# Layer 1 with one adapter per batch in four column slots, and eight value gathers moved behind the key gathers

## The chip, the core and the metric

The kernel runs on one core of one Trainium2 chip. The metric is the device time of one execution, in microseconds (us). All engines of the core work at the same time, each on its own list of instructions: TensorE (PE in the profile) for matmuls and transposes through an identity, VectorE (DVE), ScalarE (ACT), GpSimd (POOL), and SyncE (SP), which here only issues transfers. They wait for each other through semaphores.

## The reference, cut to what matters

The input x is 8 batches of 128 tokens with 512 features, in f32. Four layers follow each other, each as `x = x + ffn(cond(x))`. Layer 0 is a gated feed-forward with adapters, layer 2 an attention over a paged cache, layer 3 a routed mixture. The change lies in layer 1 and in the first steps of layer 2. Layer 1 is:

```python
B_sel = B[adapter_ids]                       # one adapter of 8 for each batch
A_sel = A[adapter_ids]
Bx  = einsum('bni,bri->bnr', x, B_sel)       # 512 features -> 16 ranks
y   = einsum('bnr,bor->bno', Bx, A_sel)      # 16 ranks -> 512, scaling 1
scores = 8 * softmax(y @ Wr.T + br)          # 8 experts, all used
low = einsum('bsd,hrd->bshr', y, A1)         # 8 experts x 16 ranks
x   = x + 2 * einsum('bshr,hor,bsh->bso', low, B1, scores)
```

In layer 2 each batch has 512 cached keys and values for each of 8 key heads, gathered row by row through a block table, and 32 query heads.

## The kernel before

The state is x, transposed: 128 partitions by 4 chunks of features by 1024 tokens. Tokens are worked on in two halves of 512 (`g` = 0, 1; `TG` = 2, and `HB` = 4 batches in each half).

**The gate stage (layer 0)** runs 11 blocks of feed-forward rows (`f` = 0 to 10, 13.4 us each). In each block, PE works through seven products for both halves, DVE and ACT evict them, POOL forms sums of the next weights (L484) after SP has loaded them (L98). Between the two parts of a block, a few prepared DVE operations are taken from generators (L615 to L617): `tables` (L200) makes index tables from the integer inputs in blocks 1 and 2, `turned_by_parts` (L360) turns weights 32 by 32 on DVE in blocks 3 to 6. What it turns is written out by SP to DRAM with the blocks exchanged and loaded back. Its scratch is rows of the big tile `h` that later blocks overwrite with their evictions. These instructions keep the order in which they are written (`kept`).

**Layer 1** does not form y. The two weights behind it that depend on no token are multiplied once into `w11` (L648): 128 rows, which are 8 adapters times 16 ranks, by 136 columns, which are 8 experts times 16 ranks and 8 router columns. Its parts, by half:

- `adapt(g)` (L771): all 8 adapters' ranks for all 512 tokens, four matmuls of 128x512 into one bank of PSUM; then DVE multiplies by `mask1` (L325, L327), which leaves for each batch the 16 rows of its own adapter and zeroes the other 112. The result is `t1`, called `l` in the profile as part of the tile `l1`.
- `mids1(g)` (L250): `t1` of each batch times `w11`, four matmuls of 128 tokens by 136 (`midp`), two in a bank, copied out by ACT (L259).
- `route1(g)`: softmax on DVE with one Exp on ACT, and the mixing weights applied (`mw`).
- `mix1(g)` (L306): four transposes on PE, copied out by ACT as `midT`.
- `outs1(g)`: four matmuls of 128x512 with `wB1` (`eo`), each added to x by DVE (L323).

Layer 0 ends with the same parts (`mix0`, `mids0`, `outs0`) and a base product, so that one of its four `eo` blocks for a half takes ten passes. The parts of both layers are interleaved by hand (L783 to L801) so that PE has work of one while DVE and ACT route the other. `small_bank` has two PSUM banks in turn and `large_bank` three.

**The attention (layer 2)** starts inside this. `att.begin` (L1365) loads weights and lets POOL gather the keys and values of step 0 (8 + 8 indirect gathers of 128 rows, L999). `att.begun` (L1372) turns those keys on DVE after the first `adapt`, and gathers the keys of step 1 into the same tiles. `att.first` (L1378) projects steps 0 and 1 with seven products each (`q_one`, `q_six`, `q_five`, L1056) and rotates the queries and keys on POOL (`vq`, `vk`, L1155) and DVE. `run` (L1408) goes over 32 steps of two batches and one key head: scores, Exp, sums, values (`av`), output product, and the projection two steps ahead. In its step 0, after the first half of the sums, it gathers the values of step 1 (L1473). POOL's instructions and those after the start of `first` keep their written order.

An f32 matmul appears in the profile as two passes.

Of the kernel before, what the change touches and what calls it, by code (L numbers as in the profile page):

```python
# [17 lines left out]
P = 128  # L18
NB = 8
# [28 lines left out]
def forward(ctx: ExitStack, tc: tile.TileContext, a: dict, out: bass.AP):  # L48
# [3 lines left out]
    def mm(o, lhsT, rhs, start, stop):  # L52
# [30 lines left out]
    down_turned, adapter_turned = (  # L83
        nc.dram_tensor(n, (rows_, P), F32, kind="Internal").ap() for n, rows_ in (("AdT", FF), ("wb1T", D))
# [109 lines left out]
    mask1 = const.tile([P, NB], F32, tag="mask1", name="mask1")  # L194
# [5 lines left out]
    def tables():  # L200
# [3 lines left out]
        yield dve.tensor_scalar(mask1, ids1, p_div16, None, ALU.is_equal)  # L204
# [34 lines left out]
    def experts(tag, wmr, topk, mult, bias, wB, base, yT, evac, mid_of=None, width=136):  # L239
# [5 lines left out]
        def operands(tok):  # L245
            if mid_of:
                return mid_of(tok)
            return [(yT[:, c, tok], wmr[:, c, :]) for c in range(DC)]

        def mids(g, bank):  # L250
            m = sm.tile([P, HB, width], F32, tag="mid", name=f"mid_{tag}_{g}")
            for j in range(HB // 2):
                ps = bank([P, 2, width], f"midp_{tag}_{g}_{j}")
                for i in range(2):
                    t0 = (g * HB + 2 * j + i) * P
                    ops = operands(slice(t0, t0 + P))
                    for k, (l, r) in enumerate(ops):
                        mm(ps[:, i, :], l, r, k == 0, k == len(ops) - 1)
                act.copy(m[:, 2 * j : 2 * j + 2, :], ps)  # L259
            M[g] = m  # L260
# [64 lines left out]
    def block_masked(dst, ps, mask, g):  # L325

        return dve.tensor_tensor(  # L327
            dst.rearrange("p (b t) -> p b t", t=P),
            ps.rearrange("p (b t) -> p b t", t=P),
            mask[:, 4 * g : 4 * g + 4].unsqueeze(2).to_broadcast([P, 4, P]),  # L330
            ALU.mult,
        )


# [6 lines left out]
    with c0:  # L341
# [18 lines left out]
        def turned_by_parts(h):  # L360

            spare = h[:, NF - 2 : NF, :].rearrange("p f t -> p (f t)")
            half = 672
# [7 lines left out]
            kept(sp.dma_start(h[:, NF - 3, 0:D], a["wb1"]))  # L371
            yield dve.transpose(h[:, NF - 3, D : 2 * D], h[:, NF - 3, 0:D])
            for q in range(4):
                kept(sp.dma_start(
                    adapter_turned.rearrange("(b i) (q j) -> q i b j", i=32, j=32)[q],
                    h[32 * q : 32 * q + 32, NF - 3, D : 2 * D].rearrange("i (b j) -> i b j", j=32),
                ))
# [235 lines left out]
        for f in range(1, NF):  # L613
            after = f + 1 < NF and weight_sums(f + 1, gate_weights(f + 1))
            gates_by_seven(f, A, itertools.chain(  # L615
                itertools.islice(tabled, 15) if f < 3 else itertools.islice(angles, 3),
                itertools.islice(turning, 3 <= f < 7),  # L617
# [134 lines left out]
    with psa:  # L752
# [13 lines left out]
        l1 = att.scratch([P, DC * P + NT], "l1")  # L766
        wa1 = l1[:, 0 : DC * P].rearrange("p (c r) -> p c r", c=DC)
        sp.dma_start(wa1, chunks(a["wa1"]))
        t1 = l1[:, DC * P : DC * P + NT]

        def adapt(g):  # L771
            tok = slice(g * 512, (g + 1) * 512)
            ps = small_bank([P, 512], f"t1_{g}")
            for c in range(DC):
                mm(ps, wa1[:, c, :], x[:, c, tok], c == 0, c == DC - 1)
            return block_masked(t1[:, tok], ps, mask1, g)
# [3 lines left out]
            mid_of=lambda tok: [(t1[:, tok], w11)],  # L780
# [8 lines left out]
        outs0(1, (0, 1), large_bank)  # L789
        adapted = adapt(0)  # L790
        outs0(1, (2, 3), large_bank)
        mids1(0, small_bank)
        route1(0)
        att.begin()
        att.begun(adapted)
        adapt(1)
        mix1(0, small_bank)
        outs1(0, range(DC), large_bank)
        mids1(1, small_bank)
# [78 lines left out]
def attention(tc, a, x, ident, lens, kvrow, part, ww, wop, ypool, sums, rot, eps, psa, c2, chunks, mm):  # L878
# [493 lines left out]
    def begun(behind):  # L1372
# [3 lines left out]
        gather(1, "k")  # L1376

# [30 lines left out]
    def run(pool_, end_of, bank, keep):  # L1408
# [20 lines left out]
        for n, (qd, p) in enumerate(steps):  # L1429
# [41 lines left out]
            if n == 0:  # L1471
# [984 lines left out]
```

## Time and profile before

| | us |
|---|---|
| median of 3 runs | 1470.01 |
| lowest, highest | 1468.61, 1470.76 |
| the profiled execution | 1471.33 |
| its span, first to last instruction | 1469.5 |
| PE busy in it | 1456.8 |
| DVE, POOL, ACT busy | 1066.5, 854.4, 557.5 |
| layer 1's first projections on PE (L53, `t`), 16 passes | 7.3 |
| its second steps (L53, `midp` from `w` and `l`), 16 passes | 2.4 |

The profile gives the start and length of each instruction, merged where equal ones follow each other ("x8"). Matmuls overlap: their mean length is longer than the distance between two starts, and what PE is held for is read from start to start. In brackets stands how long an engine stood idle before a group and what released it; "issue" means that the profile shows nothing that it waited for.

### The profile page before, as it was taken

The numbers are of one execution on the slowest core, as the hardware profiler recorded it, in microseconds if no ns is written. First come the engines' busy times: TensorE is split into PE (matmuls) and PEld (weight loads), VectorE is DVE, ScalarE is ACT, GpSimd is POOL, SyncE is SP. The second block draws the span as 40 slices with busy tenths as digits, with TensorE's granted clock in tenths as the row PEclk, the third lists the DMA queues.
The fourth block names the chain that finished last, engine by engine and source line by source line (L and its number), as shares of the span: only waits on it lengthen the run. The fifth ranks groups of instructions, "written<-read, shape, count | busy, mean of one in ns | idle before, by whom it ended". The sixth has DMA issues, their size and how long they took to land.

```text
span 1469.5 us, 17710 instructions
## 1 busy us (share of the span) xinstructions
PE 1456.8 (99%) x5313; PEld 919.3 (63%) x5313; DVE 1066.5 (73%) x2132; ACT 557.5 (38%) x1415; POOL 854.4 (58%) x877
## 2 busy tenths in 40 slices
PE   9999999999999999999999999999999999999997
PEld 7888786455555555555565555555555555557886
DVE  4675535488888887877778787777878888874575
ACT  1111101044545544454455444445544444532110
POOL 2241104477777777777677777767777776731310
PEclk9999999999999999999999999999999999999999
DMA  7430312214646544555444456445445644564001
GB/s 245 131 76 26 73 36 70 90 38 114 186 136 189 155 113 132 154 168 145 139 146 119 131 150 177 130 139 153 123 132 147 174 138 141 134 166 128 1 12 49
DMA packets 210600, 180.17 MB, mean 123 GB/s; under 512 B 85888, under 2 KB 180320, under 8 KB 210368
## 3 DMA queue, kind: packets, MB, share of 16 engines
q1 hardware_dynamic: 191888, 141.61, 34.9%
q0 software_dynamic: 17056, 36.49, 8.1%
q8 instruction: 45, 0.74, 0.2%
q10 hardware_dynamic: 1552, 0.85, 0.2%
q14 instruction: 59, 0.48, 0.1%
HBM read 133.94 MB, written 44.68 MB: 122 GB/s over the span
## 4 chain that ended last, share of the span: by engine, by line


## 5 line engine op out<-in xcount | busy, mean ns | idle before, releaser
L999 POOL DMA_INDIRECT kn<-in_k_cache,kvrow_k x256 | 271.0, 1059 | 77.5 <-issue 71.2
L999 POOL DMA_INDIRECT vals<-in_v_cache,kvrow_v x256 | 272.4, 1064 | 73.6 <-issue 60.7
L1307 PE MATMUL av<-pT,vals 128*128 128x512 f32 x640 | 290.6, 592 | 0.2 <-DVE oT L1317 0.2
L1259 ACT ACTIVATE pT<-st,hide 128x512 f32<-128x512 f32 x256 | 175.9, 687 | 190.2 <-PE st L1255 165.8
L1255 PE MATMUL st<-qT,kT 128*128 128x512 f32 x512 | 235.6, 592 | 0.0
L1307 PEld LDWEIGHTS av<-pT,vals 128*128 128x128 f32 x640 | 121.4, 190 | 153.1 <-issue 149.7
L1155 POOL TENSOR_TENSOR vq<-q,txq 128x256 f32<-128x256 f32 x128 | 121.1, 976 | 130.8 <-ACT sqq L1129 87.1
L1255 PEld LDWEIGHTS st<-qT,kT 128*128 128x128 f32 x512 | 97.1, 190 | 108.7 <-issue 105.6
L1275 DVE TENSOR_TENSOR part<-pT 128x512 f32<-128x512 f32 x128 | 88.2, 690 | 81.6 <-ACT pT L1259 70.9
L1056 PE MATMUL q_one<-q,x 128*128 128x384 f32 x256 | 93.0, 486 | 0.0
L1129 ACT ACTIVATE sqq<-q 128x128 f32<-128x128 f32 x252 | 78.3, 311 | 10.5 <-DVE q L1105 3.9
L1056 PEld LDWEIGHTS q_one<-q,x 128*128 128x128 f32 x256 | 48.5, 190 | 39.8 <-issue 14.1
L1056 PE MATMUL q_six<-q_s,xs_all 128*128 128x384 f32 x192 | 69.8, 486 | 0.0
L1110 ACT COPY q<-q_one 128x256 f32<-128x256 f32 x32 | 11.9, 372 | 151.8 <-PE q_one L1056 133.4
L1056 PE MATMUL wo_one<-o,oT 128*128 128x256 f32 x256 | 65.7, 379 | 0.0
L1255 PE MATMUL st<-qT,kTn 128*128 128x512 f32 x128 | 65.4, 592 | 0.0
L1056 PE MATMUL wo_two<-o_s,os 128*128 128x256 f32 x256 | 60.7, 380 | 0.4 <-DVE os L1015 0.4
L1259 ACT ACTIVATE pT<-st,rs 128x512 f32<-128x512 f32 x64 | 44.0, 687 | 38.6 <-PE av L1307 19.6
L484 POOL TENSOR_TENSOR ws<-wu 128x256 f32<-128x256 f32 (+1 forms) x9 | 6.4, 711 | 87.5 <-DMA wu<-in_WuT 87.5
L1056 PEld LDWEIGHTS wo_one<-o,oT 128*128 128x128 f32 x256 | 48.6, 190 | 13.5 <-issue 0.5
L1291 ACT COPY rows<-rows 32x32 f32<-32x32 f32 x96 | 20.7, 216 | 92.9 <-DVE rows L1286 67.6
L415 PE MATMUL g<-xs,ws 128*128 128x256 f32 (+1 forms) x240 | 55.1, 379 | 0.0
(460 smaller groups left out, 2795.1 us busy)
## 6 DMA issues: line engine op xcount, KB each, us to landing
turned_new<-qkt SPq DMA_DIRECT2D x120, 160.0 KB
turned_cached<-kt SPq DMA_DIRECT2D x128, 128.0 KB
kT<-turned_cached SPq DMA_DIRECT2D x32, 512.0 KB
R<-sums SPq DMA_DIRECT2D x32, 512.0 KB
qT<-turned_new SPq DMA_DIRECT2D x60, 256.0 KB
q<-in_WqT SPq DMA_DIRECT2D x8, 1024.0 KB
o<-in_WoT SPq DMA_DIRECT2D x8, 1024.0 KB
kn<-in_k_cache,kvrow_k POOLq DMA_INDIRECT x256
```

The costliest lines, as they stand in the source:

```text
L415: pe.matmul(o, lhsT, rhs, start=start, stop=stop, skip_group_check=True)
L484: kept(by.tensor_tensor(o, l, r, op))
L999: kept(pool.indirect_dma_start(out=d[:, c, :], out_offset=None, in_=kc if what == "k" else vc, in_offset=bass.IndirectOffsetOnAxis(ap=kvro ...
L1056: kept(pe.matmul(o, l[:, c, :], r[:, c, :], start=start and c == 0, stop=c == 1, skip_group_check=True))
L1110: kept(act.copy(to, ps[:, here]))
L1129: kept(act.activation(sq, S[n][m][:, j, i, :], AF.Square, accum_out=S[n]["ssq"][:, j, col : col + 1]))
L1155: kept(pool.tensor_tensor(to, t[:, b, :, hi : hi + 64], wx[:, b, lo : lo + 64].unsqueeze(2).to_broadcast(list(to.shape)), ALU.mult,))
L1255: kept(pe.matmul(ps, s["kT"][:, c, 4 * j : 4 * j + 4, :] if c < 4 else s["kn"][j][:, 0], s["qT"][j].rearrange("p a i t -> p i a t"), start ...
L1259: kept(act.activation(pT[:, c, :, :].rearrange("p i t -> p (i t)"), ps, AF.Exp, **(dict(bias=hide[:, b, c : c + 1]) if c < 4 else dict(bia ...
L1275: kept(dve.tensor_tensor(o, l, r, ALU.add))
L1291: kept(act.copy(rows[0:32, g, :], rows[32 * g : 32 * g + 32, 0, :]))
L1307: kept(pe.matmul(ps, v[:, c, :], pT[:, c, :, :].rearrange("p i t -> p (i t)"), start=c == 0, stop=c == NC - 1, skip_group_check=True,))
```

## The change

**Layer 1.** The 128 rows of the adapter weights are rearranged to four slots of 32 partitions. Slot j holds the 16 ranks of the adapter of batch j and then those of the adapter of batch 4 + j. A row number for each partition (`row1_i`, made in `tables`) does that: POOL gathers the rows of `wb1` by it directly; `wa1` is turned on DVE, written to DRAM as rows, gathered by the same numbers and turned back. `adapt(g)` then multiplies batch j of the half with the 32 columns of slot j alone, into the 32 PSUM partitions of that slot: 16 matmuls of 128 tokens, into one bank of 128x128. DVE multiplies by one scalar for each partition (`own2`), which leaves 16 rows of each 32. `mids1(g)` multiplies the 32 rows of slot j with the 32 rows of `w11` in that slot, each batch into a bank of its own (small and large in turn), with four copies on ACT. `turned_by_parts` has five turns instead of three, in blocks 3 to 7, and `wa1` is loaded from its turned form. The order of layer 1's parts among those of layer 0 is written anew.

**Layer 2.** The gathers of the values of step 1 stand right behind those of its keys, in `begun`.

```diff
@@ tables
-        yield dve.tensor_scalar(mask1, ids1, p_div16, None, ALU.is_equal)
+        yield dve.tensor_tensor(
+            of_slot.rearrange("p (s i) -> p s i", i=2), ids1.rearrange("p (i s) -> p s i", i=2),
+            block16.rearrange("p (s i) -> p s i", i=2), ALU.mult,
+        )
+        yield dve.tensor_reduce(row1, of_slot, AX.X, ALU.add)
+        yield dve.tensor_scalar(row1, row1, 16.0, p_mod16, ALU.mult, ALU.add)
+        yield dve.tensor_copy(row1_i, row1)
+        yield dve.tensor_reduce(own2, block16.rearrange("p (s i) -> p i s", i=2), AX.X, ALU.add)
@@ mids
+            if mid_into:
+                each = [bank[j % 2]([P, width], f"midp_{tag}_{g}_{j}") for j in range(HB)]
+                for j, ps in enumerate(each):
+                    mid_into(ps, g, j)
+                for j, ps in enumerate(each):
+                    act.copy(m[:, j, :], ps)
+                return
@@ turned_by_parts
+            wa, wb = (h[:, f, :] for f in (NF - 4, NF - 3))
+            def own_rows(t, src):
+                kept(pool.indirect_dma_start(
+                    out=t[:, 0:D], out_offset=None, in_=src,
+                    in_offset=bass.IndirectOffsetOnAxis(ap=row1_i[:, 0:1], axis=0),
+                ))
+            own_rows(wb, a["wb1"])
+            kept(sp.dma_start(wa[:, 0:D].rearrange("p (c r) -> p c r", c=DC), chunks(a["wa1"])))
+            t = wa[:, D : 2 * D].rearrange("p (k c j) -> p k c j", k=4, c=DC)
+            yield dve.transpose(t, wa[:, 0:D].rearrange("p (c k i) -> p k c i", c=DC, k=4))
+            for q in range(4):
+                kept(sp.dma_start(
...
             for cols in (slice(0, half), slice(half, FF)):
                 yield dve.transpose(spare[:, cols], Ad[:, cols])
...
+                if cols.start == 0:
+                    own_rows(wa, first_rows)
-            kept(sp.dma_start(h[:, NF - 3, 0:D], a["wb1"]))
-            yield dve.transpose(h[:, NF - 3, D : 2 * D], h[:, NF - 3, 0:D])
+            for t, order, home in ((wa, "p (q c j) -> p c q j", first_turned), (wb, "p (c q j) -> p c q j", adapter_turned)):
+                yield dve.transpose(
...
@@ the blocks' generators
-                itertools.islice(tabled, 15) if f < 3 else itertools.islice(angles, 3),
-                itertools.islice(turning, 3 <= f < 7),
+                itertools.islice(tabled, 17) if f < 3 else itertools.islice(angles, 3),
+                itertools.islice(turning, 3 <= f < 9),
@@ layer 1
-        sp.dma_start(wa1, chunks(a["wa1"]))
+        sp.dma_start(wa1, chunks(first_turned))
         def adapt(g):
-            ps = small_bank([P, 512], f"t1_{g}")
             for c in range(DC):
-                mm(ps, wa1[:, c, :], x[:, c, tok], c == 0, c == DC - 1)
-            return block_masked(t1[:, tok], ps, mask1, g)
+                for j in range(HB):
+                    b = g * HB + j
+                    in_slot(ps[slot(j), :], wa1[:, c, slot(j)], x[:, c, b * P : (b + 1) * P], c == 0, c == DC - 1)
+            return dve.tensor_scalar(t1[:, g, :], ps, own2[:, g : g + 1], None, ALU.mult)
...
-            mid_of=lambda tok: [(t1[:, tok], w11)],
+            mid_into=lambda o, g, j: in_slot(o, t1[slot(j), g, :], w11[slot(j), :], True, True),
...
-        outs0(1, (0, 1), large_bank)
+        outs0(1, (0,), large_bank)
         adapted = adapt(0)
-        outs0(1, (2, 3), large_bank)
-        mids1(0, small_bank)
+        outs0(1, (1,), large_bank)
+        mids1(0, (small_bank, large_bank))
         route1(0)
+        outs0(1, (2,), large_bank)
         att.begin()
         att.begun(adapted)
+        mix1(0, small_bank)
+        outs0(1, (3,), large_bank)
+        outs1(0, (0, 1, 2), large_bank)
         adapt(1)
-        mix1(0, small_bank)
-        outs1(0, range(DC), large_bank)
-        mids1(1, small_bank)
+        outs1(0, (3,), large_bank)
+        mids1(1, (small_bank, large_bank))
         route1(1)
@@ attention
         gather(1, "k")
+        gather(1, "v")
...
-            if n == 0:
-                next(sums_of)
-                gather(1, "v")
```

## The prediction

> **What bounds the kernel now.** I read the page's busy times first, then what TensorE (PE) waited for, then PE's own timeline around layer 1.
>
> ```profile
> PE 1456.8 (99%) x5313; PEld 919.3 (63%) x5313; DVE 1066.5 (73%) x2132; ACT 557.5 (38%) x1415; POOL 854.4 (58%) x877
> ```
>
> ```profile
> PE q_five L1056 <- issue: 0.7, 1, 0.7
> PE q_six L1056 <- issue: 0.6, 1, 0.6
> ```
>
> PE is busy 99% of the span at a granted clock of 0.998, and its listed waits (us in total, times, longest; the two above stand in step 2 of the attention) come to some 5 us, none above 1.2. No other engine or queue decides the end: the time is the length of PE's stream plus a few gaps. So a cut in that stream is worth its full length, unless a new wait takes its place.
>
> The stage that the change rewrites, on PE (start, length, instructions; the "x8" are four f32 matmuls, each recorded as two passes):
>
> ```profile
> 267.36 3.60 PE L53 MATMUL t<-x,l 128*128 128x512 f32 x8
> 270.79 3.60 PE L53 MATMUL eo_l<-y,base 128*128 128x512 f32 x8
> ...
> 279.38 1.09 PE L53 MATMUL midp_l<-w,l 128*128 128x136 f32 x8
> 280.53 3.70 PE L53 MATMUL t<-x,l 128*128 128x512 f32 x8
> 284.07 0.60 PE L306 MATMUL midTp_l<-ident,mw_l 128*128 128x128 f32 x4
> 285.02 0.73 PE L53 MATMUL midp_l<-w,l 128*128 128x136 f32 x4 [0.35 <-DVE l L327]
> 285.58 3.60 PE L53 MATMUL eo_l<-midT_l,wB 128*128 128x512 f32 x8
> 289.02 0.63 PE L53 MATMUL midp_l<-w,l 128*128 128x136 f32 x4
> 289.48 1.45 PE L1056 MATMUL q_one<-q,x 128*128 128x384 f32 x4
> ```
>
> Start to start, a layer-1 first projection holds PE 3.43 us (267.36 to 270.79) and 3.54 us; the second step (midp) 1.15, 0.56 and 0.46 us. Nothing else works on PE meanwhile.
>
> **What the slots cost on PE.** Removed: 2 x 4 matmuls of 128x512, 3.43 + 3.54 = 6.97 us. Added: 2 x 16 matmuls with 32 columns of weights over 128 tokens, that is 2 x 32 passes. Their like is in the trace, late in layer 2, where four column slots of 32 are also filled in turn; beside it a row-slot form of the first stage:
>
> ```profile
> 1340.02 1.31 PE L1843 MATMUL hdT<-y2T,WH 128*32 128x128 f32 x31
> 1341.05 0.39 PE L1843 MATMUL z<-y2T,A 128*32 128x256 f32 x3
> ...
> 37.36 1.03 PE L415 MATMUL g<-xs,wu 128*128 128x256 f32 x4
> 38.32 0.71 PE L415 MATMUL g<-tgm,Bg 32*128 32x256 f32 x8
> 38.85 0.61 PE L415 MATMUL g<-tum,Bu 32*128 32x256 f32 x8
> 39.39 1.13 PE L415 MATMUL g<-x,wg 128*128 128x256 f32 x4
> 40.36 1.89 PE L415 MATMUL g<-xs,ws 128*128 128x256 f32 x8
> ```
>
> 31 passes in 1.03 us, of which 0.16 was a wait of their weights for ScalarE: 28 ns each, against 108 ns for a 128x128 pass on the whole array (midTp, four in 0.43 us). So four slots run side by side. 32 passes: 0.9 us. The bound on the other side is one slot after another, 32 x 0.108 = 3.5 us, no gain at all; the hdT row is the same shape and order, so I take 0.9.
>
> **Switching the array.** The rows above show it: four passes of g take 0.86 us elsewhere (36.50 to 37.36), but 0.96 before the switch to 32 rows (37.36 to 38.32) and 0.97 after the switch back (39.39 to 40.36): 0.1 us a switch. [...] First projections: 2 x (0.9 + 0.2) = 2.2 us, saving 4.77.
>
> **The second step (midp).** Before: 1.15 + 0.56 + 0.46 = 2.17 us, and 284.07 to 285.02 is 0.95 where the transposes need 0.43: 0.52 us of waiting for L327, the mask over 128x512 (0.69 us on DVE). After: 8 passes each with 32 rows in and four different banks. tgm and tum take 0.53 us for 8 passes of 256, at a quarter of the full array's 0.216 us; for 136 columns 8 x 0.116 / 4 = 0.23 us (0.93 if the slots didn't overlap). The mask is now 128x128, some 0.28 us as the DVE copies of that size, and lies under one `eo` matmul of 0.86 us, so the 0.52 goes.
>
> New is a bank wait. In the changed program's banks, `eo` 2 of the second half goes into the bank of the second `midp`, and waits until ScalarE has copied that out; before, no such wait stood here. Only 0.2-0.3 us of matmuls cover it: results 0.3 us after the start, two copies one after the other at 0.27 us (the 128x128 copy, L1110), 0.1 us each for the hand-overs: `eo` starts about 1.05 us after the first `midp`. [...] So the first `midp` costs 0.1 + 1.05 = 1.15, no cheaper than now; the second has `q_one` in another bank behind it and costs 0.1 + 0.23 to 0.5 + 0.1, say 0.55. Together 1.70 against 2.17 + 0.52: 0.99 saved (0.5 to 1.5).
>
> Queued behind the four copies on ScalarE are the route's Exp and then `uq<-q_one`: four at 0.27 end some 0.4 us later than two at 0.39, and PE reads nothing of `uq` for over 2 us. The route (2.5 us on DVE, 280.92 to 283.42) now runs under an `eo` block of 4.29 us, after copies that end 1.5 us behind the first `midp`; its transposes start 5.3 us behind it: 1.3 us to spare. Order alone (the `eo` blocks shifted between) costs nothing on PE.
>
> **The rest, hidden.** The adapter's rows are now turned twice and gathered by POOL in the gate stage: two more 128x512 transposes on DVE (0.70 each, L372's row) in blocks 6 and 7, where DVE idles 4.36 and 3.57 us before the evictions; block 5's transpose becomes the longer one (0.90, L365's row), which makes its evictions 0.2 us later under 1.03 us of idle DVE time soon after (99.25); four more small table steps (0.2 each) in blocks 1 and 2 with 2.9 and 3.7 us idle. Two gathers on POOL, 1.06 us each by the `vals` row: the first goes ahead of a weight sum that waits 10 us for its load, the second ahead of `wds` (84.87), used on PE at 159. SP issues eight more transfers (0.5 each); those that read `h` (blocks 7 and 8) go out about 106-108 and 119-121, and what overwrites that scratch is evicted at 120.6 and 134: over 10 us to spare. Without that cover each transpose would cost 0.7 and each gather 1.1.
>
> **The moved gathers.** Eight `vals` gathers leave their place at 332.8-343.0 on POOL, behind eight `kn` gathers, and stand behind the `kn` gathers of layer 1. Queued behind them there is the first rotation, `vq`:
>
> ```profile
> 267.09 0.94 POOL L999 DMA_INDIRECT vals<-in_v_cache,kvrow_v  x1 [0.30 <-issue]
> 272.57 0.94 POOL L999 DMA_INDIRECT kn<-in_k_cache,kvrow_k  x1 [4.54 <-DVE kt L1196]
> ...
> 298.23 3.95 POOL L1155 TENSOR_TENSOR vq<-q,txq 128x256 f32<-128x256 f32 x4 [15.97 <-ACT sqq L1129]
> ```
>
> One gather takes 0.94 + 0.30 = 1.25 us. With the first projection 4.3 us earlier, the transposes that free `kn` end by 266.5, so 16 gathers run from 268.3 to 288.3. `vq` will want POOL at 298.23 - 5.8 = 292.4. The 4.1 us between hide the move: 0 here. At its old place POOL is free 10 us sooner for a rotation that isn't late: 0 again. But PE's two gaps of 0.70 and 0.63 fall there (341.9 and 344.1), while DVE stood 1.9 us with its inputs ready. No row ties that to the gathers, and blocks with such gathers later have none of it, so I keep it at 0; bounds -1.3 (gone) and +1.3 (again, elsewhere).
>
> **Sum.** 4.77 + 0.99 = 5.76 us less on PE. The profiled execution took 1471.33 (span 1469.5, 1.8 around it); it becomes 1465.6, span 1463.7. It lies 1.3 above the median, so the forecast is 1470.01 - 5.8 = 1464.2 us. About 0.2% (2.9 us) can be told from no change.
>
> **Rivals.**
> - The gaps of step 2 close too, as POOL is empty there: 5.8 + 1.3, 1462.9. For it: the place. Against: as said. 0.20.
> - New waits eat part: switches at several times 0.1 us, or copies and masks late at both second steps. 3 us kept: 1467. For it: the 1.3 us margin and the bank wait. 0.10.
> - The slots do not overlap: 1470. Against: the hdT row. 0.05.
> - Slower: the run of 16 gathers holds the first rotation. Behind `vq` come the rotated queries, ready at 307.66 on DVE and turned by PE at 309.05, 1.4 us of slack, then the first scores. Gathers at 1.25 end 4.1 us early; they cost PE time above (292.4 + 1.4 - 268.3)/16 = 1.6 us each, and undo the gain with 0.2% more above 2.14. The slowest spacing on the page is 2.33 (321.04 to 323.37). At that all 16 end at 305.6, 11.8 late: 1470 - 5.8 + 11.8 = 1476. Typical spacing speaks against. 0.05.
>
> **Chances and range.** The sum as worked out has 0.60. Faster: 0.60 + 0.20 + 0.07 of the third; same 0.08 (the rest of it and the fourth); slower 0.05. Unknowns of the likeliest: 4.8 to 6.9 us saved, 1463.1 to 1465.2. With the second case and most of the third, 1462.4 to 1467.0.
>
> **What would show it.** Two groups `t` of 32 passes about 1.1 us apart from their neighbours' starts; `eo` waiting about 0.6 us for ScalarE after the first `midp`; no wait for the mask; `vq` waiting for `q`, not for gathers; the rest of PE's timeline the same, 5.8 us earlier. Wrong: passes of `t` near 108 ns, `turned` waiting for DVE, or gaps in PE in the gate blocks 3 to 9.

## The result, and the profile after

The changed kernel takes 1476.37 us (median of 6 runs, 1475.28 to 1478.62) against 1469.55 for the kernel before (6 runs, 1468.61 to 1470.76): a ratio of 1.0049, 95% interval 1.0039 to 1.0058. It is 6.8 us slower; the forecast was 5.8 faster. The profiled execution took 1476.33, with a span of 1474.5 (before: 1469.5) and a mean granted clock of 0.994 (before: 0.998).

The page's busy times, and the longest of PE's waits (us in total, times, longest):

```profile
PE 1454.5 (99%) x5361; PEld 918.3 (62%) x5361; DVE 1066.7 (72%) x2138; ACT 557.5 (38%) x1419; POOL 857.2 (58%) x879
```

```profile
PE midp_l L799 <- DVE l L807: 9.4, 2, 7.0
...
PE eo_l L53 <- ACT mid_l L264: 0.6, 1, 0.6
```

The two waits of step 2 of the attention are gone. A new one stands in front of both second steps (`midp`): 9.4 us for the mask. PE's timeline there (start, length, instructions, the idle time ahead and its releaser):

```profile
263.03 1.08 PE L799 MATMUL t<-x,l 128*32 128x128 f32 x32
264.04 3.70 PE L53 MATMUL eo_l<-y,base 128*128 128x512 f32 x8
...
270.97 0.51 PE L799 MATMUL midp_l<-w,l 32*128 32x136 f32 x8 [2.37 <-DVE l L807]
272.06 5.40 PE L53 MATMUL eo_l<-y,base 128*128 128x512 f32 x8 [0.57 <-ACT mid_l L264]
...
285.55 1.08 PE L799 MATMUL t<-x,l 128*32 128x128 f32 x32
286.56 1.37 PE L53 MATMUL eo_l<-midT_l,wB 128*128 128x512 f32 x2
294.96 0.84 PE L799 MATMUL midp_l<-w,l 32*128 32x136 f32 x8 [7.04 <-DVE l L807]
295.73 2.93 PE L1090 MATMUL q_one<-q,x 128*128 128x384 f32 x4
```

`t` holds PE for 1.01 us, as forecast. But its mask comes late. VectorE's timeline:

```profile
270.56 0.35 DVE L807 TENSOR_SCALAR l<-t,own 128x128 f32<-128x128 f32 x1 [6.74 <-remote]
...
283.94 0.69 DVE L335 TENSOR_TENSOR x<-eo_l,x 128x512 f32<-128x512 f32 x1 [0.17 <-PE eo_l L53]
...
294.56 0.35 DVE L807 TENSOR_SCALAR l<-t,own 128x128 f32<-128x128 f32 x1 [7.96 <-remote]
```

The mask itself is short, 0.35 us. VectorE has stood idle for 6.74 and 7.96 us, with its other instructions in order behind this one, and starts 6.5 us after the first `t` ended (264.1) and 8.0 us after the second (286.6). In the program, this instruction waits for TensorE's counter (a semaphore) alone. "Remote" means that this counter was raised just before the start, and that no instruction of the trace ended shortly before that. The trace also records when the counter is raised, though some entries are missing: after 263.11 the next one is at 270.54, and after 284.77 at 294.53, that is, 0.02 and 0.03 us before the two masks start. TensorE had gone on to its next matmuls at 264.04 and 286.56. This speaks for a late word of TensorE and against a slow VectorE. (The ends of matmuls are modelled in the profile; whether the last results were late as well can't be seen.) Nor does the trace show a load of instructions there: the two queues that the page lists as "instruction" (q8 with 45 packets, q14 with 59) have no packet in either stretch (the nearest start at 249.4, 273.1 and 307.7). GpSimd, at the same time, is in the gathers:

```profile
267.46 0.94 POOL L1033 DMA_INDIRECT vals<-in_v_cache,kvrow_v  x1 [0.30 <-issue]
271.80 0.94 POOL L1033 DMA_INDIRECT kn<-in_k_cache,kvrow_k  x1 [3.40 <-DVE kt L1230]
...
281.79 0.94 POOL L1033 DMA_INDIRECT vals<-in_v_cache,kvrow_v  x1 [0.30 <-issue]
...
290.53 0.94 POOL L1033 DMA_INDIRECT vals<-in_v_cache,kvrow_v  x1 [0.30 <-issue]
306.71 3.96 POOL L1189 TENSOR_TENSOR vq<-q,txq 128x256 f32<-128x256 f32 x4 [15.23 <-ACT sqq L1163]
```

One run of gathers ends at 268.40 and the first mask starts 2.16 us later; the next ends at 291.47 (290.53 + 0.94) and the second mask starts 3.09 us later. The rotation `vq` did not wait for the gathers: it starts at 306.71, 15.2 us after them, behind `sqq`. (The gathers of the keys of step 1 start at 271.80 and not near 268.3 as forecast: they wait for `kt` on VectorE, which stands behind the late mask.)

The rest of the loss is the clock. The timeline in stretches (busy time of each engine, then the granted clock, the DMA share and GB/s):

```profile
core 0: us, PE busy (x) PEld busy (x) DVE busy (x) ACT busy (x) POOL busy (x), PEclk, DMA share, GB/s
264.00:268.00 4.00, 4.00 (x14) 1.82 (x10) 0.00 (x0) 0.00 (x0) 3.08 (x4) 1.00 0.18 59
...
273.00:276.00 3.00, 3.00 (x5) 1.19 (x4) 1.68 (x7) 0.23 (x1) 2.34 (x3) 0.53 0.76 192
277.00:286.00 9.00, 9.00 (x40) 4.13 (x42) 3.24 (x6) 0.58 (x1) 6.87 (x8) 1.00 0.55 184
...
291.00:295.00 4.00, 0.04 (x4) 0.04 (x4) 0.44 (x2) 0.00 (x0) 0.47 (x1) 0.50 0.10 33
295.00:300.00 5.00, 5.00 (x15) 2.93 (x16) 3.59 (x12) 1.51 (x6) 0.00 (x0) 0.50 0.00 0
301.00:303.00 2.00, 2.00 (x7) 1.14 (x6) 1.32 (x3) 0.00 (x0) 0.00 (x0) 1.00 0.00 0
```

After each of the two waits PE runs at half its clock (0.50) for some us. The `eo` behind the first takes 5.40 us instead of 3.60 (+1.8); the second `midp` +0.3, `q_one` 2.93 instead of 1.45, and the `q_six` behind it 2.46 instead of 1.56. Together 4.5 us. The record of the clock says the same: it is at 0.50 from 273.16 to 276.58 and from 290.23 to 300.47, PE works 8.9 us of that, and half of it is lost. Waits of 9.4 and clock of 4.5 make 13.9 us. The first scores of the attention (`st`) start at 321.20 instead of 312.72, 8.5 us later; so 13.9 - 8.5 = 5.4 us were saved in PE's stream up to there, close to the 5.76 of the forecast. Of the 8.5 us, 2.0 come back in step 2, whose two gaps are gone (scores behind it at 371.82 instead of 365.31).

### The profile page after: what moved, and what is told of

Same layout as the page of the kernel before. It is cut to its first block, busy times and chain, and to the rows that moved or that the text cites. A ratio compares the mean times of both kernels' runs of the same rounds, so it can differ in the third digit from the quotient of the medians.

```text
span 1474.5 us, 17837 instructions
## 1 busy us (share of the span) xinstructions
PE 1454.5 (99%) x5361; PEld 918.3 (62%) x5361; DVE 1066.7 (72%) x2138; ACT 557.5 (38%) x1419; POOL 857.2 (58%) x879
## 4 chain that ended last, share of the span: by engine, by line
## 5 line engine op out<-in xcount | busy, mean ns | idle before, releaser
L1090 PEld LDWEIGHTS q_one<-q,x 128*128 128x128 f32 x256 | 49.0, 192 | 40.4 <-issue 15.2
```

Source lines behind the costliest of these rows:

```text
L1090: kept(pe.matmul(o, l[:, c, :], r[:, c, :], start=start and c == 0, stop=c == 1, skip_group_check=True))
```

## The experiments

All kernels were timed beside the kernel before on the same chip, and each ratio is to that kernel. The chips are named by number, since it turned out to matter. "Held" stands for a word of TensorE that comes microseconds late.

**What holds the mask?** Four one-edit kernels on chip 13, where the kernel before takes 1469.45 us.

The mask as a product of two tensors, without an operand that is one scalar for each partition:

```diff
-            return dve.tensor_scalar(t1[:, g, :], ps, own2[:, g : g + 1], None, ALU.mult)
+            return dve.tensor_tensor(t1[:, g, :], ps, own2[:, g : g + 1].to_broadcast([P, P]), ALU.mult)
```

> The changed kernel with one instruction in another form: the mask l is the product of two tensors (the column own2 spread over 128 tokens by a zero step) and not a product with a per-partition scalar. Everything else, the moved gathers too, stays. Theory A (the per-partition scalar, read from SBUF, cannot be fetched while GpSimd runs its gathers back to back): both waits of l (6.74 and 7.96 us on VectorE, 2.37 and 7.04 us on TensorE) go, and the slow clock behind them; what was forecast for the change comes out, 1463.7 us (1462.4 to 1465.5). Theory B (the end of a projection in slots reaches VectorE late, whatever instruction waits for it): nothing changes, 1476 us, l again about 7 us after t. Theory C (sixteen gathers in a row load the DMA engines or GpSimd so that anything near them is late): 1475 to 1477 us, the wait of the second l stays.

1476.23 us, ratio 1.0045 [1.0031, 1.0058]; VectorE still idles 6.41 and 8.02 us ahead of the masks. So it is not that operand. The same with a constant in the scalar's place (it leaves out the masking by adapter):

```diff
-            return dve.tensor_scalar(t1[:, g, :], ps, own2[:, g : g + 1], None, ALU.mult)
+            return dve.tensor_scalar(t1[:, g, :], ps, 1.0, None, ALU.mult)
```

> The changed kernel with the mask multiplied by the constant 1.0, which is in the instruction, in place of the per-partition scalar own2: the same operation of VectorE, the same shape, no scalar to fetch. It leaves out the masking by adapter. Theory A in the form 'the scalar's fetch is what waits': both waits go, the time is within 1 us of the product of two tensors, 1463.7 us. Theory A in the form 'this kind of operation on VectorE is held, whatever its scalar': the waits stay, 1476 us. Theory B: the waits stay.

1476.87 us (one run), waits of 6.34 and 7.96 us: the same.

The gathers of the values put back to their old place in step 0 of the attention:

```diff
         gather(1, "k")
-        gather(1, "v")
...
             summed(n, 0)
+            if n == 0:
+                next(sums_of)
+                gather(1, "v")
```

> The changed kernel with only the gathers of the second step's values back at their old place; the slots and the mask with a per-partition scalar stay. Theory A: the gathers of the keys end near 281.5 us, the second projection t ends near 286, so the second l waits for nothing; the first l, at the values of the first step, still waits about 6.7 us on VectorE and TensorE 2.4 us for it. TensorE gains 7.0 us of waiting and about 2.6 us of slow clock behind it; the two gaps of step 2 (1.3 us) come back: 1476.4 - 9.6 + 1.3 = 1468.1 us (1466.5 to 1469.5). Theory B: both waits stay, 1476 us or more. Theory C: the second wait goes, as with A.

1466.90 us (19 runs), ratio 0.9983 [0.9976, 0.9990]. The gathers of the keys end at 281.4, before the second `t` (285.38), and its mask follows at 286.52 without a wait. The first stays late (270.43) and costs PE 1.77 us of idle time: its gathers, of step 0, are where they were. And the kernel before with the move alone:

```diff
         gather(1, "k")
+        gather(1, "v")
...
-            if n == 0:
-                next(sums_of)
-                gather(1, "v")
```

> The kernel before with only the gathers moved: layer 1 as it was, its mask a product of two tensors of 128x512. Theory A: a product of two tensors is not held by gathers, so l is made 0.1 us after t as before; the gaps of 0.70 and 0.63 us in step 2 go as they did in the changed kernel: 1468.2 us (1467.4 to 1469.6). Theory C: the second l is held until the sixteen gathers are through near 292 us, some 8 us, and the time is 1474 to 1478 us. Theory B says nothing of it (no slots): 1469.5 us.

1477.44 us, ratio 1.0057 [1.0044, 1.0071]: no slot is needed, the move alone costs 8.0 us. Here other signals of TensorE come late as well, one of them to ScalarE. VectorE's timeline in this kernel, then ScalarE's, then PE's:

```profile
287.30 0.69 DVE L327 TENSOR_TENSOR l<-t,mask 128x512 f32<-128x512 f32 x1 [3.28 <-remote]
```

```profile
290.87 0.58 ACT L308 COPY midT_l<-midTp_l 128x512 f32<-128x512 f32 x1 [8.43 <-remote]
```

```profile
284.68 0.60 PE L306 MATMUL midTp_l<-ident,mw_l 128*128 128x128 f32 x4
288.05 0.90 PE L53 MATMUL midp_l<-w,l 128*128 128x136 f32 x4 [2.77 <-issue]
291.50 4.71 PE L53 MATMUL eo_l<-midT_l,wB 128*128 128x512 f32 x6 [2.56 <-ACT midT_l L308]
```

The four transposes end at 285.3, and ScalarE copies them out at 290.87. PE goes on 0.06 us after the mask's end and 0.05 us after the copy's: signals the other way are prompt here. So what is late in this trace is TensorE's word that it has finished, to VectorE (2.5 us: `t` ends at 284.8, its mask starts at 287.30) and to ScalarE (5.6 us, 285.3 to 290.87), and of the two kernels only the one with the moved gathers shows it.

**What in the gathers?** On chip 15, where the kernel before takes 1468.29 us. The values of step 1 gathered ahead of the keys, the same gathers in one unbroken run:

```diff
-        gather(1, "k")
         gather(1, "v")
+        gather(1, "k")
```

> The changed kernel with the two groups of gathers of step 1 in the other order: the eight of the values first, the eight of the keys behind them. The theory of the operand (A) and the theory of the slots (B) have fallen; what is left is that TensorE's signals reach VectorE and ScalarE late while GpSimd gathers. Theory D: what counts is the place in an unbroken run of gathers (from about the ninth on), not what they fetch: signals stay prompt until about 282 us, the second l waits as before, some 8 us, and the time is 1475 to 1478 us. Theory E: it is the gathers of the values themselves (other table, other target): the hold moves to 272 to 282 us, the copy of midTp near 279 us and the additions to x wait, the second l does not, and the time is 1470 to 1476 us.

Plain transfers by SyncE in the place of the values' gathers of steps 0 and 1 (they fetch rows 0 to 511 and leave out the page table):

```diff
+                if what == "v" and n < 2:
+                    sp.dma_start(d[:, c, :], vc[c * P : (c + 1) * P, :])
+                    continue
                 kept(pool.indirect_dma_start(
```

> [...] Theory D or E (GpSimd's gathers are what delays TensorE's signals): both l come 0.1 us after t, nothing of the 9.4 us of waiting is left, 1463.5 us (1462 to 1466). Theory F (traffic on the DMA engines delays them): l stays late, 1472 us or more.

The gathers back, the first projection of the slots sent one `eo` block later, and the second one ahead of layer 1's four `eo` blocks for the first half, no longer behind three of them:

```diff
-        outs0(1, (0,), large_bank)
+        outs0(1, (0, 1), large_bank)
         adapted = adapt(0)
-        outs0(1, (1,), large_bank)
+        outs0(1, (2,), large_bank)
...
-        outs0(1, (2,), large_bank)
...
+        outs0(1, (3,), large_bank)
         mix1(0, small_bank)
-        outs0(1, (3,), large_bank)
-        outs1(0, (0, 1, 2), large_bank)
         adapt(1)
-        outs1(0, (3,), large_bank)
+        outs1(0, range(DC), large_bank)
```

> The changed kernel with the gathers back at their old place (as in the run before with 1466.9 us) and the first projection t in slots one output chunk later, behind chunks 0 and 1 of the second group: TensorE then has 4.6 us of chunk 2 to do until the first l is there (270.4 us in that run), and chunk 3 goes in front of the transposes. Theory D or E: l comes at about 270.4 us whatever the place of t, no wait of TensorE is left (1.77 us), nor the slow clock behind it (1.75 us on one chunk): 1463.4 us (1462 to 1465). If the signal is late by a fixed 6 us wherever it is sent, l comes at 274 to 275 us and the time is 1465.5 to 1468 us.

And a pause between keys and values, of 20 small memsets on GpSimd:

```diff
+    rest = ap.tile([P, 160], F32, tag="rest", name="rest")
...
         gather(1, "k")
+        for _ in range(20):
+            kept(pool.memset(rest, 0.0))
         gather(1, "v")
```

> [...] The run of sixteen is cut into two of eight. Theory D (place in an unbroken run): the second l, due near 286.6 us, comes at once, the 7 us of TensorE's waiting go, 1467 to 1470 us. Theory E (the gathers of the values as such): if they are going on at 287 us, l waits for them to end, and with the later end (296 to 300 us) the wait is longer than 8 us, 1480 us or more.

They took 1463.00 (one run), 1463.86 (0.9968 [0.9957, 0.9979]), 1463.12 (0.9962 [0.9948, 0.9976]) and 1464.96 us (one run), and none of them showed a late mask: each starts within 0.1 us of the end of its `t` (263.99 and 282.38, 263.78 and 282.16, 268.93 and 280.44, 264.73 and 283.11). But the first of them has as long a run of gathers as any, 32 from 247.1 to 288.5, and its masks stand in the middle of it. So this chip (on which the changed kernel itself was not run) could not tell the theories apart, and the same kernels went to others.

> The changed kernel once more, unaltered, side by side with the one that gathers the values first. Up to the first l the two have the same instructions on TensorE, VectorE, ScalarE and GpSimd, and yet l waited 6.7 us in the one and 0.1 us in the other; the two were not measured side by side. Theory D' (what GpSimd has queued decides, keys before values holds the signals): 1476 us again, both l late. Theory G (the hold belongs to the chip or its state at the time and not to the kernel): 1463 us, both l prompt.

> The changed kernel with the gathers of the values of step 1 in front of those of its keys, as in the single run with 1463.0 us, now timed in rounds. Theory D': 1463 us (1462 to 1465), whatever the changed kernel beside it does. Theory G: the same time as the changed kernel beside it, within 1 us, fast or slow.

On chip 5 the changed kernel takes 1476.62 us (before: 1470.75), and the kernel with the values first, which took 1463.00 on chip 15, takes 1478.84: ratio 1.0057 [1.0040, 1.0074]. VectorE's first mask on chip 15, and on chip 5:

```profile
263.99 0.35 DVE L807 TENSOR_SCALAR l<-t,own 128x128 f32<-128x128 f32 x1 [0.35 <-PE t L799]
```

```profile
281.56 0.35 DVE L807 TENSOR_SCALAR l<-t,own 128x128 f32<-128x128 f32 x1 [17.78 <-remote]
```

The same instruction of the same program, its input ready at 263.9 and 264.1: once 0.1 us later, once 17.5 us later, which is 3.6 us after the end of 24 gathers in a row (247.2 to 278.0). The record of TensorE's counter has the word at 263.97 on chip 15 and at 281.54 on chip 5. So the hold is not in the program alone: it was there on chip 5 and not on chip 15, be it for the chip or for its state at the time. Chip 13 holds it, so the three other kernels were run there, beside the changed one (the kernel before then took 1469.60).

> The changed kernel for the third time, as the mark beside which the next three are read: two kernels with the same instructions up to the first l gave 1463 and 1478 us when run at different times, so that the hold hangs on the chip or its state. If the hold is there, 1476 us and l about 7 us late twice; if it is not, 1463 to 1465 us and both l 0.1 us behind t.

> The kernel with 16 plain transfers by SyncE in place of GpSimd's gathers of the values of steps 0 and 1 (rows 0 to 511 are fetched: it leaves out the page table for these values), now beside the changed kernel. If GpSimd's gathers are what holds TensorE's signals: 1463.9 us whether the changed kernel beside it is held or not. If the hold is in the DMA traffic or in nothing that the kernel does: as late as the changed kernel.

> The kernel with the gathers at their old place and the first t in slots one chunk later, now beside the changed kernel. If the changed kernel is held: l sent at 268.9 us comes when the gathers of step 0 are through, near 270.4 us, inside the chunk of 4.6 us that follows; the second l meets only the last of the gathers of the keys; 1463 to 1465 us plus the two gaps of step 2 (1.3 us) if they are held as before. If a hold is 6 to 8 us wherever it strikes: 1467 us or more.

> The kernel with some 5.7 us of small memsets of GpSimd between the gathers of the keys and of the values of step 1, now beside the changed kernel. If the changed kernel is held and what counts is an unbroken run of gathers: the first l is late as there (2.4 us of waiting and the slow clock behind it), the second l is not, 1467 to 1470 us. If any gather holds the signals: the second l waits for the end of the values, later than in the changed kernel, 1479 us or more. Not held: 1465 us as in the single run.

The changed kernel: 1475.57 us, masks 6.4 and 7.9 us late. The plain transfers: 1463.02, ratio 0.9961 [0.9946, 0.9975]. VectorE in these two:

```profile
269.75 0.35 DVE L807 TENSOR_SCALAR l<-t,own 128x128 f32<-128x128 f32 x1 [6.42 <-remote]
293.70 0.35 DVE L807 TENSOR_SCALAR l<-t,own 128x128 f32<-128x128 f32 x1 [7.92 <-remote]
```

```profile
263.68 0.35 DVE L807 TENSOR_SCALAR l<-t,own 128x128 f32<-128x128 f32 x1 [0.35 <-PE t L799]
282.06 0.35 DVE L807 TENSOR_SCALAR l<-t,own 128x128 f32<-128x128 f32 x1
```

With GpSimd's sixteen gathers of the values replaced, both masks are on time and 12.5 us are saved. SyncE sends its transfers early, from 239.3 to 251.1, and the remaining gathers, of keys, end at 256.96 and 274.61, so that neither `t` ends among gathers. The load of the DMA engines is not the cause here: other transfers keep them full (a DMA share of 1.04, 402 GB/s) just when the second `t` ends, at 281.99,

```profile
280.00:282.00 2.00, 2.00 (x36) 1.04 (x34) 1.72 (x3) 0.00 (x0) 0.00 (x0) 1.00 1.04 402
```

and its mask starts at 282.06, while in the changed kernel the first mask is held at a DMA share of 0.18 and 59 GB/s (264 to 268 above). With the pause: 1467.44, ratio 0.9987 [0.9978, 0.9996]. GpSimd and VectorE there:

```profile
280.23 0.94 POOL L1034 DMA_INDIRECT kn<-in_k_cache,kvrow_k  x1 [0.30 <-issue]
281.16 5.74 POOL L1413 MEMSET rest<- 128x160 f32 x20
287.06 1.08 POOL L1034 DMA_INDIRECT vals<-in_v_cache,kvrow_v  x1 [0.16 <-issue]
```

```profile
270.25 0.35 DVE L807 TENSOR_SCALAR l<-t,own 128x128 f32<-128x128 f32 x1 [6.16 <-PE eo_l L53]
284.68 0.35 DVE L807 TENSOR_SCALAR l<-t,own 128x128 f32<-128x128 f32 x1
```

The second `t` ends at 284.6, within the pause, and its mask is on time although GpSimd is just as busy; the first has no pause and is late. So in this run it is gathering, and not a GpSimd busy for 5.74 us with other work. The gathers back with later slots: 1465.34, ratio 0.9971 [0.9960, 0.9982]; the first mask is late as well (269.78, for a `t` that ends at 268.0) but lies under an `eo` block now; the second, for a `t` sent within the gathers of the keys, starts at 282.47, 2.9 us late.

**Does the form of the signal matter?** On chip 0, where the kernel before takes 1469.19 us: the changed kernel as a mark, the slots projected one after another with a mask for each (so that TensorE signals after at most five matmuls, not sixteen), and the kernel before with its unslotted `adapt(0)` one block earlier.

> The changed kernel once more, only as the mark for the two beside it: held, 1476 us and l some 7 us late twice; not held, 1463 to 1465 us. Both theories expect either.

```diff
-            for c in range(DC):
-                for j in range(HB):
...
-            return dve.tensor_scalar(t1[:, g, :], ps, own2[:, g : g + 1], None, ALU.mult)
+            for j in range(HB):
+                b, s = g * HB + j, slot(j)
+                for c in range(DC):
+                    in_slot(ps[s, :], wa1[:, c, s], x[:, c, b * P : (b + 1) * P], c == 0, c == DC - 1)
+                done = dve.tensor_scalar(t1[s, g, :], ps[s, :], own2[s, g : g + 1], None, ALU.mult)
+            return done
```

> The changed kernel with each projection t done slot after slot (four matmuls of one slot, then the next) and masked in four pieces of 32x128, so that TensorE signals after 5 matmuls at most and not once after 16. The slots then hardly overlap: t is dearer, up to 3.5 us in place of 1.0. If it is the signal behind 16 matmuls that GpSimd's gathers hold: the pieces of l come at once, 1463 us plus 2 times 2.5 us = 1468 us. If it is the slots, or the place in the run of gathers: the first piece of l is as late as l is in the changed kernel beside it (if that is held), 1478 us or more.

```diff
-        outs0(1, (0, 1), large_bank)
+        outs0(1, (0,), large_bank)
         adapted = adapt(0)
-        outs0(1, (2, 3), large_bank)
+        outs0(1, (1, 2, 3), large_bank)
```

> The kernel before, its whole projection t in one 128x512 group as it was, with the first one an output chunk earlier: it ends near 266.6 us, while the gathers of the values of step 0 go on until 268 us; nothing else is moved. If the slots or the signal behind 16 matmuls make the hold: l comes at 266.7 us and the time stays at 1469.6 us within 1 us. If the hold strikes any projection whose end falls into the gathers (and the kernel before was spared because its first t ended at 270.9 us, behind them): l comes at 270.2 us or later; TensorE has two chunks of eo to do until 272 us, so the time is also about 1469.6 us: the time does not tell, the start of l does.

The mark: 1475.02 us, held. Slot by slot: 1487.05, ratio 1.0117 [1.0101, 1.0134]; the second piece of the first mask comes at 269.44 after 4.59 us of idle time, and one of the second half at 298.49 after 5.66, so the number of matmuls behind a signal is not it. The kernel before with `adapt(0)` earlier: 1471.58, ratio 1.0017 [1.0009, 1.0024]. Its first mask was on time, in the middle of the gathers (247.6 to 278.9); the additions behind it were not:

```profile
267.13 0.69 DVE L327 TENSOR_TENSOR l<-t,mask 128x512 f32<-128x512 f32 x1 [2.74 <-PE t L53]
277.28 0.69 DVE L323 TENSOR_TENSOR x<-eo_l,x 128x512 f32<-128x512 f32 x1 [8.24 <-issue]
282.22 1.29 DVE L323 TENSOR_TENSOR x<-eo_l,x 128x512 f32<-128x512 f32 x2 [4.25 <-PE midp_l L53]
```

PE finished the `eo` of the first addition near 271.3, 6.0 us before VectorE took it up. So a signal of full-array matmuls came late within the gathers too, while another in the same run of gathers did not (the mask at 267.13, less than 0.1 us after its `t`): what decides which is not settled by these runs.

**A version that bears the hold.** The gathers at their old place; the first `t` one `eo` block later, so that a late mask is covered; the transposes of the first half (`mix1`) put inside the fourth `eo` block; and the second `t`, as in the changed kernel, behind three of the four `eo` blocks of layer 1, now beyond the end of the keys' gathers:

```diff
-        def outs(g, os, bank):
+        def outs(g, os, bank, between=None):
...
+                if between:
+                    between()
...
-        outs0(1, (0,), large_bank)
+        outs0(1, (0, 1), large_bank)
         adapted = adapt(0)
-        outs0(1, (1,), large_bank)
+        outs0(1, (2,), large_bank)
...
-        outs0(1, (2,), large_bank)
...
-        mix1(0, small_bank)
-        outs0(1, (3,), large_bank)
+        outs0(1, (3,), large_bank, lambda: mix1(0, small_bank))
```

> The changed kernel with the gathers of the second step's values back at their old place, with the second half of adapt(0) (the y side's projection) put inside the fourth chunk of outs1, after its eight matmuls of the base weight, and with t(1) sent behind three chunks of outs1(0). Theory, signals of TensorE sent during a long run of gathers are held to a little after its end: on a chip that holds, t(1) is sent near 282.5 us, some 1.6 us after the last gather of the keys (280.9 us with one set of gathers less in front), so its mask is there within 1 us and midp_l(1) waits for nothing that shows; no wait above 1 us for l, and 1463.3 us (1462.5 to 1465.0). On a chip that does not hold: the same TensorE work, 1463.1 us. Rival, the hold strikes this signal wherever it is sent: l(1) is 2 to 3 us late, part of it seen at midp_l, and 1465.5 us or more.

On chip 7: 1463.39 us against 1469.24, ratio 0.9960 [0.9946, 0.9973]. VectorE, then PE:

```profile
270.80 0.35 DVE L809 TENSOR_SCALAR l<-t,own 128x128 f32<-128x128 f32 x1 [2.62 <-remote]
...
283.61 0.35 DVE L809 TENSOR_SCALAR l<-t,own 128x128 f32<-128x128 f32 x1 [0.23 <-PE t L801]
```

```profile
267.38 1.08 PE L801 MATMUL t<-x,l 128*32 128x128 f32 x32
...
273.65 0.51 PE L801 MATMUL midp_l<-w,l 32*128 32x136 f32 x8
...
282.38 1.08 PE L801 MATMUL t<-x,l 128*32 128x128 f32 x32
283.39 1.12 PE L53 MATMUL eo_l<-midT_l,wB 128*128 128x512 f32 x2
284.44 0.51 PE L801 MATMUL midp_l<-w,l 32*128 32x136 f32 x8
```

This chip holds too: the first mask is 2.3 us late, 2.5 us after the last gather of step 0 (268.28). It costs `midp` nothing, as PE comes to it at 273.65. The second `t` ends 1.3 us after the last gather of the keys (282.11), and its mask follows 0.2 us later. The later slots with the gathers back gave 1465.34 on chip 13; that was another chip, and the intervals of the two ratios overlap, so it is not shown that this order is worth more than that one.

**PE itself.** In three traces of chips that hold, PE also stands still by itself while a mask is late: 1.54 us in the changed kernel on chip 5, 0.74 and 0.81 us on chip 0, and 0.61 us in the last version, each before a matmul of `eo` for which the profile shows no wait:

```profile
288.79 0.59 PE L53 MATMUL eo_l<-midT_l,wB 128*128 128x512 f32 x1 [1.54 <-issue]
```

So it need not be the word alone that is held up; what stops PE there was not tested.

## Why the prediction was wrong

**First projections, 4.77 us: right.** 1.01 us each instead of 1.1 (263.03 to 264.04, 285.55 to 286.56); 6.97 - 2.02 = 4.95 saved. The slots do run side by side (32 passes in 1.01 us, 32 ns each with both switches of the array in it, against 108 ns for a pass of the transposes at 278.15), and so a switch cost no more here than the 0.1 us read off the gate stage.

**The rest, hidden: right.** The gate stage lost nothing: PE's first projection follows an `eo` that starts at 262.08 instead of 262.21.

**Second steps, 0.99 us: right in kind.** On the chip that holds nothing (values first), they take 1.08 us (268.35 to 269.43) and 0.45 (283.29 to 283.74): 1.53 where 1.70 was forecast, the bank wait for ScalarE (0.57) included. From the end of the first `eo` block of layer 0's second half to `q_one`, PE needs 20.9 us there (262.85 to 283.74) against 26.4 before (263.07 to 289.48): 5.5 us saved of the 5.76 of the sum. The time agrees, 1463.00 (one run) against 1468.29. So the sum on PE was sound, and on such a chip the forecast would have come true.

**"The mask lies under one `eo` matmul of 0.86 us, so the 0.52 goes": this step failed.** It took for granted that VectorE learns of the end of `t` at once, as it did in the profile of before (L327 started within 0.2 us of its `t`). In the changed kernel it learns of it 6.5 and 8.0 us later. The first `t` had been moved to 263, into the gathers of the values of step 0 that run to 268.4, and its cover cut from two `eo` blocks to one (4.6 us, from 264.04 to 268.60): 2.37 us of wait. The second has 1.4 us of cover: 7.04.

**"The moved gathers: 0": this step failed, and it is the larger one.** It asked only what is queued behind the gathers on GpSimd, and for that it was right: `vq` waited for ScalarE, not for them. The cost lies with VectorE and ScalarE, which wait for TensorE meanwhile, and with PE behind them. The move alone costs 8.0 us; undoing it in the changed kernel brings 1475.57 down to 1466.90 on the same chip, 8.7 us. The bounds of ±1.3 us were drawn from two gaps of PE in step 2, and these look like the same hold: in the profile of before, the `uq` that follows `q_five` starts 2.7 us after its matmuls end (339.3), within the old gathers of step 1's values, and the trace has TensorE's counter raised at 341.95 (VectorE's timeline of the kernel before):

```profile
339.52 0.55 DVE L1069 TENSOR_TENSOR uq<-q_six,uq 128x384 f32<-128x384 f32 x1
341.97 0.56 DVE L1071 TENSOR_TENSOR uq<-q_five,uq 128x384 f32<-128x384 f32 x1 [1.90 <-PE q_one L1056]
```

The prediction saw that VectorE "stood 1.9 us with its inputs ready", found no row that tied this to the gathers, and set it to nothing. It was a delay of 2.7 us in a place where other work covered most of it. Moved to a place where PE waits for each signal, the gathers cost 8.0 us, six times those two gaps.

**The clock was left out.** An idle PE was priced at its idle time. The 9.4 us of waiting brought 4.5 us more at half the clock.

**The rivals.** That the gaps of step 2 close (0.20) did happen, but also in kernels that leave the gathers at their old place (gathers back on chip 13, the last version on chip 7), so it was not the empty place that closed them. New waits at both second steps (the third, 1467) was the right place with the wrong price: late copies and masks were to take 2.8 us of the gain, and the masks alone, with the clock behind them, came to 13.9. The slower one (0.05) named the run of 16 gathers, with the wrong victim; its 1476 us agrees with the result by accident, since no gather was slower than 0.95 us there.

**What is shown and what is not.** Shown: the time is lost between the end of TensorE's matmuls, as the profile gives it, and the start of the engine that waits for them, and the entries of TensorE's counter come just ahead of that start; on chip 13, which holds, the masks were on time where GpSimd's gathers were replaced (263.68 and 282.06), paused (284.68) or moved (286.52), and neither 5.74 us of other work of GpSimd nor a DMA share of 1.04 held one; the hold stayed with another operand of the mask (6.41 and 8.02 us), without slots (the move alone) and with fewer matmuls behind a signal (4.59 and 5.66 us); chips 5, 13, 0 and 7 hold, 15 did not in four kernels. Most of the held signals came 1.4 to 3.6 us after the last gather of a run, a few inside the run. The packets of a gather go on after its end in GpSimd's timeline, but this is not the whole delay: those of step 0's last gather ran from 269.14 to 269.58, after its end at 268.40, and the first mask started 1.0 us after them; for the second mask it is 1.9 us (292.67 to 294.56), for the one on chip 5 2.4 us (279.18 to 281.56). By which path the gathers and the late word hang together, and why some signals pass inside a run, stays open. The clock's share (4.5 us) is read from the trace; no kernel here took the waits' length away and left the halved clock.

## What to carry to other kernels

Ask of a long run of GpSimd's gathers not only what is queued behind it on GpSimd, but which engines wait for TensorE's results meanwhile: here such a signal was up to 17.5 us late. What helped here was cover (a mask 2.3 us late cost the last version's `midp` nothing), a place beyond the end of the run (the mask there followed its `t` within 0.2 us) and a run broken up (the second mask of the pause, on time). Ask also after a wait that the profile puts down to "remote" or "issue" with its input ready for microseconds, however small it is where it stands: the two gaps of 0.70 and 0.63 us in step 2 stood beside the gathers whose move cost 8.0. Look at what the other engines do at that moment before moving that work elsewhere. Price an idle PE with the clock behind it (4.5 us behind 9.4 here), and run an explanation on a second chip before it is believed (1463.00 and 1478.84 for one kernel here).

## What was not expected of the hardware

- Signals from TensorE came late within a run of GpSimd's indirect gathers (1.25 us each, from start to start) or up to 3.6 us behind it: to VectorE by up to 17.5 us (values first on chip 5), to ScalarE by 5.6 us (the move alone, chip 13). From VectorE or ScalarE to TensorE nothing was late (0.05 to 0.06 us, in the rows shown).
- The same program took 1463.0 us on one chip (one run) and 1478.8 on another, 1.1% apart, where the kernel before differed by 0.2% (1468.3 and 1470.8).
- The granted clock fell to 0.50 after PE had stood still for as little as 1.77 us (gathers back, 269.07 to 270.84; at 0.50 from 271.88 to 275.29). In the changed kernel, 2.37 us were followed by 0.50 from 273.16 to 276.58, and 7.04 us by 0.50 from 290.23 to 300.47, 5.5 us beyond the restart: 3.4 us and three times that. Idle times of 1.17 us (later slots) and of 1.27 and 1.80 us (pause; behind the longer one, 268.85 to 270.65, an `eo` took 3.70 us, where the one in gathers back took 5.35) were followed by none. So no length of idle time can be read off these runs as the one that decides.
